# Two bottleneck blocks on one core: the second tile of block one's first convolution computed by seven half-size products inside the stream, in place of eight whole ones ahead of it

## The chip, the cores and the metric

The kernel runs on one core of one Trainium2 chip. The metric is the device time of one execution in microseconds (us); the median of several runs is compared. Engines are named as in the profile: PE (matrix products), PEld (weight loads into PE), DVE (vector), ACT (scalar activation), POOL, and SP, which here only issues transfers. All data is float32.

## The reference, cut to what matters

Two residual blocks of the same form, one after the other, on 64 images of 1024 channels and 14 x 14 pixels. The change lies in the first 1x1 convolution of block one.

```python
def block(x, w1, b1, g1, be1, w2, b2, g2, be2, w3, b3, g3, be3, residual_scale):
    out = relu(_bn(_conv(x, w1, b1, 1, 0), g1, be1))      # 1x1, 1024 -> 256 channels
    out = relu(_bn(_conv(out, w2, b2, 1, 1), g2, be2))    # 3x3, 256 -> 256
    out = _bn(_conv(out, w3, b3, 1, 0), g3, be3)          # 1x1, 256 -> 1024
    return relu(x + softplus(residual_scale)[0] * out)
x = block(x, L0 weights); x = block(x, L1 weights)
```

`_bn` normalizes each channel by its mean and variance over all images and pixels, so a convolution has to be finished on all images before what follows it can start.

## The kernel before, in words

**Tiles.** The images are taken two at a time: 32 tiles (`T`), each with 8 slices of 128 channels and 392 pixels (`PX`, the columns of a matmul). A tile is 1.6 MB and is loaded whole with one transfer (`load_x`, L104); tile zero comes in eight pieces and tile one in two. Tiles alternate between two pools of two buffers each, `x_right` and `x_left`: tiles 0 and 1 right, 2 and 3 left, 4 and 5 right, and so on. A load of a tile therefore waits until the tile four places before it has been read for the last time.

**Two ways to do the first convolution.** The 1x1 convolution is a product of a 256 x 1024 matrix with a 1024 x 392 tile. `plain_conv1` (L653) does it as eight block products: two halves of the output channels times eight slices of input channels, 16 matmuls of 392 columns. `Conv1` (L341, a `Seven`, L245) does a 2 x 2 block product with seven products in place of eight: the blocks are the two halves of output channels, the two halves of input channels, and two blocks of columns. With two tiles in a unit the blocks of columns are the two tiles, and `n` is 392; with one tile they are its two halves, and `n` is 196. Each product is four matmuls of `n` columns. For that, four sums of the weights are made once (`combine_w1`, L145; on DVE at L140) and, for each unit, four sums of the input blocks on DVE (`t3`, `t2`, `t1` in `after1`, L436, and `t4` in `after6`, L455). The seven products are `p1` to `p7`. `p1` and `p2` need no sum; `p6` needs `t2`, `p5` needs `t1`, `p7` needs `t3`, `p4` needs `t4`. Results are put together on DVE (L427) with the help of copies on ACT (L332), and DVE takes the statistics (L430).

**Order.** `stream` (L288) interlocks units: a unit's `p4` and `p3` come after the next unit's `p1`. For the first unit the order is p1, p2, p6, p5, p7; for a later one p1, then the last two of the unit before, then p6, p2, p5, p7. Matmuls, ACT work and filter steps keep the order in which they are written; where the other DVE work and the transfers go, a scheduler decides when the program is built. Between products `stream` calls `beside`, three times in the first unit and six times in a later one. Each call takes some steps of `filters` (L167), which transforms the 3x3 filters of both blocks in eight pieces of nine steps: it loads a piece (`load`, L182; the transfer is issued on SP at L185), forms sums on DVE (L192, L195), scales them on ACT and writes them to memory from POOL (L206). `calls` spreads the steps over 66 calls, eleven units' worth.

**The start.** Weights and the first tiles are loaded, the small per-channel parameters are prepared, three matmuls without use (`busy`) run, then tiles zero and one by `plain_conv1`, then 15 units of two tiles by `stream`. The last unit leads over into the 3x3 convolution (`closing`, L384). Behind it come the second convolution and the rest of both blocks, which the change leaves as they are.

Of the kernel before, what the change touches and what calls it, by code (L numbers as in the profile page):

```python
# [10 lines left out]
FP = mybir.dt.float32  # L11
# [3 lines left out]
P = 128  # L15
# [3 lines left out]
CS = C // P  # L19
MS = M // P  # L20
G = 2
T = N // G
PX = G * HW
# [46 lines left out]
def bottlenecks(ctx: ExitStack, tc: tile.TileContext, x, w1s, w2s, w3s, pars, out):  # L70
# [15 lines left out]
    def two(t, s):  # L86

        j = t % (GI // G)
        return y_grp[:, s, t // (GI // G), :, j * G * W : (j + 1) * G * W]

    class Psum:


        def __init__(self, scope, cycle, **bufs):
            self.pool = scope.enter_context(
                tc.tile_pool(name="psum", bufs=1, space=bass.MemoryType.PSUM, reuse_waits="tile")
            )
            self.cycle, self.bufs = itertools.cycle(cycle), bufs
# [17 lines left out]
    def load_w1(pool, b, queue):  # L116

        w = pool.tile([P, MS, 2, CS // 2, P], FP, tag="w1", name=f"w1_{b}")
        n = CS // 2
        for h, o in itertools.product(range(2), range(MS)):  # L120

            step = n // 2 if b == h == o == 0 else n
            for s in range(0, n, step):
                queue.dma_start(out=w[:, o, h, s : s + step], in_=w1s[b][:, o, h, s : s + step])
        return w
# [19 lines left out]
    def combine_w1(w, s):  # L145
        return combine([[w[:, o, h] for h in range(2)] for o in range(MS)], s)
# [10 lines left out]
    def matmul(*args, **kw):  # L157

        tc.keep_in_program_order(nc.tensor.matmul(*args, **kw))  # L159

    def busy(psum, tag, n, with_=None):

        v = ident if with_ is None else with_
        for i in range(n):
            matmul(psum.tile(448, tag), v, v[:, :1].to_broadcast([P, 448]), start=True, stop=True)
# [79 lines left out]
    class Seven:  # L245


        border = None
# [39 lines left out]
    def stream(items, total, beside=lambda: None, together=False):  # L288


        before = ahead = None
        items = iter(items)
        for k in range(1, total + 1):
            now = ahead if k == 2 and together else next(items)
            if k == total and now.border is not None:
                yield from now.closing(before)
                return
            if k == 1 and together:
                ahead = next(items)
                for part in now.p1, ahead.p1, now.p2, now.p6, now.p5, ahead.p6, now.p7:  # L300
                    yield from part()
                before = now
                continue
            if now is not ahead:
                yield from now.p1()
            if before is not None:
                beside()
                yield from before.last()
                beside()
            else:  # L310
                yield from now.p2()
            if now is not ahead:
                yield from now.p6()
            if before is not None:
                before.end()
                if k < total:
                    beside()
                    yield from now.p2()
            beside()
            yield from now.p5()  # L320
            beside()
            yield from now.p7()
            beside()
            if k == total:
                yield from now.p2()
            before = now
        yield from before.last()
        before.end()

    def act(*args, **kw):  # L330

        tc.keep_in_program_order(nc.scalar.activation(*args, **kw))  # L332
# [8 lines left out]
    class Conv1(Seven):  # L341
# [2 lines left out]

        prefix = "a"

        def __init__(self, psum, pool, xs, ts, w1, par, stats, border, at=None):
            self.psum, self.pool, self.ts, self.par, self.stats = psum, pool, ts, par, stats
            self.at = at = at or ts
            self.border = border if at[-1] == T - 1 else None  # L350
            self.pinned = at[-1] >= T - 1 - len(ts)
            self.a, self.s = w1
            self.n = n = len(xs) * PX // 2
            px = [slice(0, n)] * 2 if len(xs) == 2 else [slice(0, n), slice(n, 2 * n)]
            self.b = [
                [xt[:, h * CS // 2 : (h + 1) * CS // 2, p] for xt, p in zip((xs[0], xs[-1]), px)] for h in range(2)
            ]

        def sum(self, i):
            return self.pool.tile([P, CS // 2, self.n], FP, tag=f"at{i}", name=f"at{i}")  # L360

        def product(self, bank, w, b, start):
            n = CS // 2
# [2 lines left out]
                yield  # L366

        def saved(self, tag, bufs=1):
            v = self.pool.tile([P, self.n], FP, tag=tag, name=tag, bufs=bufs)
            act(v, self.y, AF.Copy)  # L370
            return v

# [110 lines left out]
    class Conv3(Seven):  # L483
# [25 lines left out]
        def part(self, row, i):  # L509
            return self.xt[:, self.o[row], i * self.n : (i + 1) * self.n]  # L510
# [150 lines left out]
    def plain_conv1(psum, t, xt, a, par, stats):  # L661

        banks = [psum.tile() for o in range(MS)]
        for h in range(2):
            for o, ps in enumerate(banks):
                for s in range(CS // 2):
                    matmul(ps, a[o][h][:, s], xt[:, h * CS // 2 + s], start=h + s == 0, stop=h + s == CS // 2)
        for o, ps in enumerate(banks):
            y = two(t, o)
            nc.scalar.activation(  # L670
                y, ps.rearrange("p (h l) -> p h l", h=H), AF.Identity, bias=par[:, B1 + o : B1 + o + 1]
            )
            nc.vector.bn_stats(stats[:, o, t, :], y)
# [1219 lines left out]
    def stats_tile(n, name):  # L1893
        return keep.tile([P, n, T, nc.vector.BN_STATS_DIM], FP, tag=f"stats{n}", name=name)
# [148 lines left out]
    par = []  # L2043
    stats1 = stats_tile(MS, "stats1_0")
# [6 lines left out]
    with tc.tile_pool(name="first", bufs=1) as one, tc.tile_pool(  # L2051
        name="first_x", bufs=2
    ) as x_left, ExitStack() as scope:
        xpools = x_right, x_left
        psum = Psum(scope, ["ps"], ps=4, ay=2)
        for i in range(1, 3):
            one.tile([P, CS // 2, PX], FP, tag=f"at{i}", name=f"at{i}")
        w1 = load_w1(one, 0, nc.scalar)
        pair = [load_x(x_right, 0, t, CS if t == 0 else 2) for t in range(2)]
        for b in range(2):  # L2060
            p = keep.tile([P, NPAR], FP, tag=f"par{b}", name=f"par{b}")
            nc.scalar.dma_start(out=p, in_=pars[b][:, :NPAR])
            par.append(p)
        sps = [softplus(p) for p in par]
        nc.scalar.activation(small.tile([P, 1], FP, tag="root", name="root"), sps[1], AF.Sqrt)
        masks.make_identity(nc, ident)
        busy(psum, "ps", 3, ones)
        w1, summed = combine_w1(w1, sums_tile(one, 1)[:, 0])
        for _ in summed:
            pass  # L2070

        border = Border(0, stats1, x_scope)
        for t, xt in enumerate(pair):
            plain_conv1(psum, t, xt, w1[0], par[0], stats1)


        spare = [y_all[:, i, NPX - CS * PX :] for i in range(MS)]
        pieces = list(itertools.product(range(2), range(MS), range(MS)))
        work = filters(pieces, spare)
        total, calls, count = FSTEPS * len(pieces), 6 * (T // 2 - 1 - CS // MS), itertools.count(1)  # L2080

        def beside():
            i = next(count)
            for _ in itertools.islice(work, total * i // calls - total * (i - 1) // calls):
                pass

        def items():
            for t in range(2, T, 2):
                xs = [load_x(xpools[t // 2 % 2], 0, t + i) for i in range(2)]
                yield Conv1(psum, one, xs, (t, t + 1), w1, par[0], stats1, border)  # L2090

        for _ in stream(items(), T // 2 - 1, beside):
            pass

    for b in range(2):
# [9 lines left out]
        with tc.tile_pool(name=f"last_{b}", bufs=1, **({"reuse_waits": "tile"} if b == 0 else {})) as one, tc.tile_pool(  # L2105
            name=f"last_x_{b}", bufs=2 if b == 0 else 5
# [3 lines left out]
            if b == 0:  # L2110
                w1, ws_a = load_w1(one, b + 1, nc.sync), sums_tile(one, 1)
# [6 lines left out]
            with ExitStack() as scope:  # L2118
                if b == 0:
                    psum = Psum(scope, ["cy"], cy=2, ay=2)  # L2120
                else:
                    psum = Psum(scope, ["cy", "cx"], cy=2, cx=2, cp=2)
# [3 lines left out]
                with tc.tile_pool(name=f"gram_{b}", bufs=1) as pool:  # L2126
                    if b == 0:
                        xs, places = [], positions()
# [9 lines left out]
                    else:  # L2138
                        homes = [x_left.tile([P, CS * PX], FP, tag="x", name="home") for _ in range(3)]
                        total = NPX // (CH * P)  # L2140
                        beside = {total - 14 + 2 * i: partial(next, summed) for i in range(4)}
# [17 lines left out]
                else:  # L2159
                    xs = [load_x(x_left, b, t, run=tc.keep_in_program_order) for t in range(5)]  # L2160
# [5 lines left out]
                with tc.tile_pool(name=f"rest_{b}", bufs=1) as pool:  # L2166
# [3 lines left out]
                    stats1 = stats_tile(MS, f"stats1_{b + 1}")  # L2170
                    border = Border(b + 1, stats1, x_scope)
# [41 lines left out]
```

## Time and profile before

| | |
|---|---|
| median of 3 runs | 1896.02 us (1895.59 to 1896.64) |
| the profiled execution | 1896.71 us, of which 1894.6 us are the span of the profile |
| PE busy, share of the span | 1876.6 us, 99% |
| DVE busy | 1574.0 us, 83% |
| ACT busy | 1092.0 us, 58% |
| POOL busy | 748.4 us, 40% |
| first matmul of tile zero | 5.72 us from the start of the span |
| first matmul of the pair 2, 3 | 27.44 us |
| first matmul of the pair 4, 5 | 40.61 us |

Times of single instructions are counted from the start of the span. A product of the program is one matmul; in the trace it is two passes, each with a weight load (PEld) of its own, so counts of PE are twice those of the code. Line numbers with an L are those of the kernel before. In a line of the timeline stand the start, the duration (or the stretch, where a line merges several), the engine, the line and the operation, the tile written and the tile read, and in brackets the idle time of the engine before and what ended it. `SPq` is SP issuing a transfer; the time is that of the issue, not of the transfer.

### The profile page before, as it was taken

What the parts mean: (1) busy time and instruction counts of PE and PEld (TensorE: products, weight loads), DVE (VectorE), ACT (ScalarE), POOL (GpSimd) and SP (SyncE); (2) the same over time, 40 slices, a digit from 0 to 9 for tenths busy, and PEclk for the clock granted to TensorE, in tenths of its full rate; (3) what the DMA queues carried; (4) which work ended last, traced back from release to release, by engine and by line L of the source; (5) the groups of instructions that cost most, each with busy time, mean ns of one, the idle gap of its engine ahead of it and who ended that gap; (6) DMA issues with size and microseconds to landing.
All of it is one profiled execution on the core that took longest, in us unless ns stands there. A gap on an engine that the chain in (4) does not pass through costs nothing. (4 is left out here: it accounts for less than half of the span.)

```text
span 1894.6 us, 28577 instructions
## 1 busy us (share of the span) xinstructions
PE 1876.6 (99%) x9778; PEld 1563.6 (83%) x9778; DVE 1574.0 (83%) x2484; ACT 1092.0 (58%) x2275; POOL 748.4 (40%) x764
## 2 busy tenths in 40 slices
PE   9999999999999999999999999999999999999999
PEld 5555557999997998899999999999999986555555
DVE  5787867999998776778878788799999986888886
ACT  2222214677777665555555555457777692666666
POOL 0111100121206555377676776501121141666665
PEclk9999999999999999999999999999999999999999
DMA  7777654797764555678788889459788467799997
GB/s 288 271 252 258 223 184 131 206 217 219 206 201 161 181 177 204 248 272 308 279 278 309 281 302 285 193 168 223 212 208 226 141 160 289 262 346 345 334 354 270
DMA packets 262369, 458.19 MB, mean 242 GB/s; under 512 B 59152, under 2 KB 228976, under 8 KB 249040
## 3 DMA queue, kind: packets, MB, share of 16 engines
q1 hardware_dynamic: 224160, 373.28, 58.8%
q0 software_dynamic: 31216, 28.81, 7.8%
q10 hardware_dynamic: 6848, 54.28, 7.1%
q8 instruction: 78, 1.28, 0.3%
q14 instruction: 67, 0.55, 0.1%
HBM read 289.44 MB, written 141.03 MB: 227 GB/s over the span
## 5 line engine op out<-in xcount | busy, mean ns | idle before, releaser
L332 ACT ACTIVATE x<-x,shift 128x392 f32<-128x392 f32 x452 | 260.0, 614 | 77.2 <-DVE x L514 31.5
L159 PE MATMUL columns<-v,ub 128*128 128x224 f32 (+1 forms) x1536 | 302.5, 338 | 1.3 <-ACT columns L332 0.8
L159 PEld LDWEIGHTS columns<-v,ub 128*128 128x128 f32 x1536 | 268.8, 188 | 7.5 <-ACT columns L332 1.5
L332 ACT ACTIVATE cu<-cy,scale 128x196 f32<-128x196 f32 (+1 forms) x360 | 175.4, 499 | 166.5 <-PE cy L159 158.9
L159 PE MATMUL ay<-at,ws 128*128 128x196 f32 (+1 forms) x768 | 192.7, 382 | 1.4 <-DVE at L440 1.4
L159 PEld LDWEIGHTS ay<-at,ws 128*128 128x128 f32 x768 | 136.1, 190 | 36.5 <-issue 1.9
L514 DVE SCALAR_TENSOR_TENSOR x<-cp,scale,x 128x196 f32<-128x196 f32 (+1 forms) x240 | 124.6, 519 | 46.1 <-PE cp L159 44.7
L645 POOL TENSOR_TENSOR x<-x,cu 128x392 f32<-128x392 f32 x120 | 125.6, 1047 | 73.3 <-DVE x L514 72.1
L332 ACT ACTIVATE au<-ay 128x196 f32<-128x196 f32 (+1 forms) x140 | 53.8, 384 | 171.8 <-PE ay L159 157.8
L159 PE MATMUL l<-diffs,ub 128*128 128x224 f32 (+1 forms) x768 | 150.2, 338 | 0.3 <-ACT sd L1934 0.3
L159 PE MATMUL m<-sums,ua 128*128 128x224 f32 (+1 forms) x752 | 145.9, 336 | 0.0
L159 PEld LDWEIGHTS l<-diffs,ub 128*128 128x128 f32 x768 | 135.2, 190 | 1.3 <-ACT sd L1934 0.6
L159 PEld LDWEIGHTS m<-sums,ua 128*128 128x128 f32 x752 | 131.5, 189 | 0.8 <-DVE sums L761 0.2
L1059 POOL DMA_DIRECT2D y<-f x24 | 32.7, 1688 | 233.7 <-DVE f L979 233.7
L537 POOL TENSOR_TENSOR x<-x,cu 128x196 f32<-128x196 f32 (+1 forms) x120 | 105.1, 875 | 47.7 <-ACT cu L332 26.2
L159 PE MATMUL cx<-y,w 128*128 128x196 f32 (+1 forms) x396 | 122.2, 394 | 1.2 <-ACT cx L332 1.2
L159 PE MATMUL cy<-y,w 128*128 128x196 f32 (+1 forms) x372 | 117.0, 402 | 0.7 <-DVE y L1461 0.7
L542 POOL TENSOR_TENSOR x<-x,cu 128x392 f32<-128x392 f32 x60 | 79.2, 1320 | 84.9 <-DVE x L514 80.7
L332 ACT ACTIVATE y<-y,shift,scale 128x1568 f32<-128x1568 f32 (+7 forms) x94 | 106.7, 1153 | 7.8 <-DVE shift L1966 6.5
L206 POOL DMA_DIRECT2D u<-y x48 | 26.0, 543 | 212.4 <-ACT y L332 211.6
L940 ACT ACTIVATE columns<-m 128x448 f32<-128x448 f32 (+1 forms) x144 | 70.8, 492 | 58.8 <-PE m L159 54.0
L1825 POOL TENSOR_SCALAR y<-y,scale 128x392 f32<-128x392 f32 x57 | 92.4, 1622 | 28.8 <-DVE scale L2156 28.2
(303 smaller groups left out, 4556.6 us busy)
## 6 DMA issues: line engine op xcount, KB each, us to landing
ub<-u SPq DMA_DIRECT2D x92, 768.0 KB, 5.2
x<-in_x SPq DMA_DIRECT2D x35, 1568.0 KB, 8.0
mid<-x ACTq DMA_DIRECT2D x32, 1568.0 KB, 9.2
x<-mid SPq DMA_DIRECT2D x32, 1568.0 KB, 9.1
out<-x SPq DMA_DIRECT2D x123, 392.0 KB, 6.9
x<-in_x SPq DMA_DIRECT2D x108, 392.0 KB, 7.8
ua<-u SPq DMA_DIRECT2D x92, 256.0 KB, 3.0
z<-kept SPq DMA_DIRECT2D x60, 392.0 KB, 3.0
```

What stands on the lines that cost most here:

```text
L159: tc.keep_in_program_order(nc.tensor.matmul(*args, **kw))
L206: nc.gpsimd.dma_start(out=us[b][i][:, s, o], in_=u)
L332: tc.keep_in_program_order(nc.scalar.activation(*args, **kw))
L514: run(nc.vector.scalar_tensor_tensor(v, bank, self.scale[:, o : o + 1], v, ALU.mult, ALU.add))
L537: run(nc.gpsimd.tensor_add(self.part(1, 1), self.part(1, 1), u3))
L542: run(nc.gpsimd.tensor_add(v, v, self.u12))
L645: nc.gpsimd.tensor_add(v, v, self.u12[:, i * self.n : (i + 1) * self.n])
L940: copy(v, m, AF.Copy)
L1059: nc.gpsimd.dma_start(out=out_rows[3][:, o], in_=fa[:, o, :full], accum_op=ALU.add)
L1825: run(nc.gpsimd.tensor_scalar(z, z, scale[:, o : o + 1], None, ALU.mult))
```

## The change

Tile one leaves `plain_conv1` and becomes the first unit of the stream: a `Conv1` of one tile, whose two blocks of columns are the tile's halves of 196. The stream now has 16 units in place of 15. Its buffers keep the size that they have for a pair (`width`), and only the first 196 columns of each are used. The rest of the stream is written as before, but since units are counted from tile one, the calls of `beside` that fell beside the pair 2, 3 now fall beside tile one, those of the pair 4, 5 beside the pair 2, 3, and so on.

```diff
-        def __init__(self, psum, pool, xs, ts, w1, par, stats, border, at=None):
+        def __init__(self, psum, pool, xs, ts, w1, par, stats, border, at=None, width=None):
...
             self.n = n = len(xs) * PX // 2
+            self.width = width or n
...
         def sum(self, i):
-            return self.pool.tile([P, CS // 2, self.n], FP, tag=f"at{i}", name=f"at{i}")
+            return self.pool.tile([P, CS // 2, self.width], FP, tag=f"at{i}", name=f"at{i}")[:, :, : self.n]
...
         def saved(self, tag, bufs=1):
-            v = self.pool.tile([P, self.n], FP, tag=tag, name=tag, bufs=bufs)
+            v = self.pool.tile([P, self.width], FP, tag=tag, name=tag, bufs=bufs)[:, : self.n]
...
-        for t, xt in enumerate(pair):
-            plain_conv1(psum, t, xt, w1[0], par[0], stats1)
+        plain_conv1(psum, 0, pair[0], w1[0], par[0], stats1)
...
         def items():
+            yield Conv1(psum, one, pair[1:], (1,), w1, par[0], stats1, border, width=PX)
             for t in range(2, T, 2):
...
-        for _ in stream(items(), T // 2 - 1, beside):
+        for _ in stream(items(), T // 2, beside):
             pass
```

## The prediction

> **What bounds the kernel now.** I read the page first: its head, the busy shares, the clock in slices and the chain.
>
> ```profile
> span 1894.6 us, 28577 instructions
> PE 1876.6 (99%) x9778; PEld 1563.6 (83%) x9778; DVE 1574.0 (83%) x2484; ACT 1092.0 (58%) x2275; POOL 748.4 (40%) x764
> ...
> PEclk9999999999999999999999999999999999999999
> ...
> PE 34%; DMA 0%; DVE 0%; SPq 0%; ACT 0%; issue 0%; DVEq 0%
> ```
>
> PE is busy for 99% of the span at the full clock, and whatever the chain names is PE. So time changes by what PE works less, plus what PE newly waits. A late PE in this stage is late to the end, since the order of its work behind the change stays the same. Next, the timeline of the first 45 us: start, duration, engine, tile written<-read, and in brackets what ended the idle time before.
>
> ```profile
> 0.76 10.13 SPq L109 DMA_DIRECT2D x<-in_x  x12
> ...
> 10.93 1.20 SPq L185 DMA_DIRECT2D y<-in_w  x2
> ...
> 13.09 0.69 DVE L140 TENSOR_TENSOR ws<-w 128x512 f32<-128x512 f32 x1
> ...
> 15.02 0.69 DVE L140 TENSOR_TENSOR ws<-w,ws 128x512 f32<-128x512 f32 x1
> ...
> 23.39 1.79 DVE L439 TENSOR_TENSOR at<-x 128x1568 f32<-128x1568 f32 x1 [5.09 <-DMA x<-in_x]
> ...
> 25.10 1.78 DVE L441 TENSOR_TENSOR at<-x,x 128x1568 f32<-128x1568 f32 x1
> 26.80 0.56 DVE L673 BATCH_NORM_STATS2 stats<-y 128x6 f32<-128x392 f32 x1
> ...
> 27.28 1.77 DVE L440 TENSOR_TENSOR at<-at,x 128x1568 f32<-128x1568 f32 x1
> 27.44 2.80 PE L159 MATMUL ay<-x,w 128*128 128x392 f32 x8
> ...
> 32.71 2.80 PE L159 MATMUL ay<-at,ws 128*128 128x392 f32 x8
> ...
> 40.61 2.80 PE L159 MATMUL ay<-x,w 128*128 128x392 f32 x8
> ```
>
> PE runs without a wait here, but the loads run hardly ahead of it. DVE sits idle until 23.39 for the load of tile three. Its three sums for the first pair (L439, L441, L440) end at 29.05, and PE reads the third at 32.71: 3.7 us of slack. The changed program uses more than that.
>
> **The change, part by part.** *Products.* A matmul stands in the trace as two passes (x counts passes). Two stretches without idle time give the price, one of 392 columns and one of 196.
>
> ```profile
> core 0: us, PE busy (x) PEld busy (x) DVE busy (x) ACT busy (x) POOL busy (x), PEclk, DMA share, GB/s
> 200.00:300.00 100.00, 100.00 (x305) 57.72 (x304) 64.56 (x85) 18.98 (x37) 6.44 (x12) 1.00 0.51 184
> 1000.00:1100.00 100.00, 100.00 (x604) 99.66 (x604) 81.80 (x155) 56.63 (x128) 69.99 (x57) 1.00 0.81 286
> ```
>
> 392 columns: 100 / 152.5 = 0.656 us. 196 columns: 100 / 302 = 0.331 us; weight loads (PEld) fill that stretch too, but add nothing. Tile one now costs 16 x 0.656 = 10.50 us, so it starts at 27.44 - 10.50 = 16.94. It will cost 28 x 0.331 = 9.27: **1.23 us less**.
>
> *What moves.* The instruction order of the built programs, engine by engine, differs in one stretch of PE, and on SP and DVE up to tiles 20 and 25; POOL is the same. What matters:
>
> ```
> PE   tile 1: p1 p2 p6 p5 p7 | pair 2,3: p1 | tile 1: p4 p3 | pair 2,3: p6 p2 p5 p7
> SP   before: x_1 x_2 x_3 in_w in_w x_4      after: x_1 in_w in_w x_2 x_3 x_4
> DVE  after: ... L428 (tile 1), L192, L440 L442 L441 (tile 3: t3, t1, t2), ...
> ```
>
> The filter steps start one unit earlier, because tile one is now the stream's first unit, and their two first loads now stand ahead of tiles two and three. (L440, L442, L441 are L439, L441, L440 of before.) I asked the DMA view for stretches that hold one issue each, and the timeline for the issue times; the last column is us to landing.
>
> ```profile
> 9.75 0.43 SPq L109 DMA_DIRECT2D x<-in_x  x1
> 10.22 0.66 SPq L109 DMA_DIRECT2D x<-in_x  x1
> 11.53 0.61 SPq L185 DMA_DIRECT2D y<-in_w  x1
> ...
> x<-in_x SPq DMA_DIRECT2D x1, 784.0 KB, 6.5
> x<-in_x SPq DMA_DIRECT2D x1, 1568.0 KB, 9.8
> x<-in_x SPq DMA_DIRECT2D x1, 1568.0 KB, 13.1
> y<-in_w SPq DMA_DIRECT2D x1, 576.0 KB, 13.9
> y<-in_w SPq DMA_DIRECT2D x1, 576.0 KB, 14.7
> ```
>
> Tile one's second half (issued near 9.4) lands at about 15.9, tile two at 9.75 + 9.8 = 19.6, tile three at 10.22 + 13.1 = 23.3, the filter loads at 10.93 + 13.9 = 24.8 and 11.53 + 14.7 = 26.2. They land in the order of issue, back to back, so the swap leaves the sum as it is: tile two should land at 19.6 + (26.2 - 23.3) = 22.5 and tile three at **26.2**.
>
> *PE up to the new wait.* Tile one from 16.94: 20 matmuls to 23.56; p1 of the pair (needs tile two, 22.5) to 26.18; tile one's p4 and p3 to **28.83**. Then p6 of the pair needs t2. DVE starts t3 when tile three lands; from the start of L439 to the end of L440, without the 0.48 us that L673 takes between, are 29.05 - 23.39 - 0.48 = 5.18 us. So t2 is ready at 26.2 + 5.2 = 31.4, and **PE waits 2.6 us**, from 28.83 to about 31.45. If tile three still landed at 23.4, t2 would be there at 28.6 and the wait would be nothing.
>
> *The two together.* p6, p2, p5, p7 take 16 x 0.656 = 10.50 from 31.45: p1 of pair 4,5 starts at 41.95, where it started at 40.61. **+1.3 us**, gain included. What stands before p6 cancels out unless it exceeds 2.6 us.
>
> *Waits inside tile one.* Its sums have 784 elements:
>
> ```profile
> L439 DVE TENSOR_TENSOR at<-x 128x784 f32<-128x784 f32 x32 | 54.3, 1696 | 0.0
> L440 DVE TENSOR_TENSOR at<-at,x 128x784 f32<-128x784 f32 x32 | 40.2, 1258 | 1.1
> L441 DVE TENSOR_TENSOR at<-x 128x784 f32<-128x784 f32 x32 | 31.2, 975 | 0.0
> ```
>
> The weight sums on L140 now end near 16.7 (15.7 plus t1's 1.0); then t3 (1.7), one L673 (0.5) and t2 (1.3) end at 20.2, against p6 of tile one at 16.94 + 8 x 0.331 = 19.6. A wait of 0 to 0.6 us, inside the 2.6: no cost. Behind t2 of the pair DVE has L192, statistics, L428 and t4; p5, 5.2 us after p6, needs the L428 that empties its bank, about 1.9 us of DVE work away: no cost. Loads: tile five waits on tile one's last product, so is issued near 28.8 in place of 27.6 and, at the 7.3 us that one took, lands at 36; its sums start when p5 has ended, past 39. Third and fourth filter loads wait on DVE steps that now come a unit earlier, with the same steps per unit: nothing, within the one wait on DVE that this stage has:
>
> ```profile
> PE ap L159 <- DVE y L427: 0.8, 1, 0.8
> ```
>
> It can go, or come twice: -0.8 to +0.8.
>
> *The clock.* This cost isn't in the sum of busy times. The waits list gives the longest waits of PE, and narrow windows the granted clock (third last column) around two of them.
>
> ```profile
> PE columns L159 <- DVE sums L761: 2.5, 2, 1.9
> PE cx L159 <- ACT cx L332: 1.2, 1, 1.2
> ...
> 598.00:600.00 2.00, 0.81 (x6) 0.79 (x6) 1.73 (x4) 1.73 (x5) 1.90 (x3) 1.00 0.97 301
> 600.00:602.00 2.00, 1.87 (x11) 1.57 (x11) 1.12 (x4) 1.49 (x5) 1.84 (x3) 1.00 0.78 252
> 1236.00:1238.00 2.00, 0.76 (x3) 0.04 (x1) 1.88 (x4) 0.68 (x2) 0.00 (x0) 1.00 0.48 160
> 1238.00:1240.00 2.00, 1.29 (x5) 1.22 (x6) 1.82 (x11) 0.70 (x3) 0.14 (x2) 0.81 1.05 339
> 1240.00:1242.00 2.00, 2.00 (x7) 1.82 (x6) 1.97 (x6) 1.77 (x3) 0.00 (x0) 0.50 1.00 344
> 1242.00:1244.00 2.00, 2.00 (x10) 1.91 (x10) 1.86 (x4) 0.57 (x4) 0.00 (x0) 0.84 0.25 89
> ```
>
> A wait of 1.2 us near 599 left the clock at 1.00. One of 1.9 us near 1237 was followed by half clock: the missing 0.19 + 0.50 + 0.16 of 2 us each, doubled, are 3.4 us at half speed, 1.7 us of work lost. Our wait of 2.6 us is longer, so I expect one such dip; part of it may fall on the wait's own end. Bounds 0 and 1.7; I take **1.5**.
>
> The Trainium skill, "TensorE: Matmul & The Clock Gate", "HAM oscillation — how this bites in real kernels", gives as the abstract rule no PE-idle gaps over about 3.4 us. By it a wait of 2.6 us would keep the clock, and the sum would end at +1.3. The dip after 1.9 us at 1237 speaks against that bound; the page's own window of 3413 ns agrees with the dip's length of 3.4 us.
>
> **Sum.** -1.23 + 2.6, rounded to +1.3, + 1.5 = +2.8 to +2.9 us. The profiled execution took 1896.71 us, 2.1 around its span of 1894.6; the median of the three runs is 1896.02. The change touches nothing around the span, so I set the sum on the median: **1898.9 us** (1899.6 on the profiled execution). About 0.2%, 3.8 us, is what a measurement of this kernel can tell from no change.
>
> **Rivals.**
>
> *B, the wait without the dip: 1896.02 + 1.3 = 1897.4.* For it: the 1.2 us wait at 599 cost no clock; a 2.6 us wait that a monitoring interval's edge halves looks like two of 1.3. Against: 1.9 us sufficed at 1237. (The skill's rule named above would lead here too.)
>
> *C, tile three isn't late: 1896.02 - 1.23 = 1894.8.* If transfers don't go strictly by issue, or the swapped loads share the engines, tile three could land near 23.4, and PE would not wait; each us of earlier landing below 26.2 gives back one. Against: the landings above keep the order of issue.
>
> *D, the loads are slower than the swap says: clearly slower.*
>
> ```profile
> 0.00:20.00 20.00, 18.93 (x48) 10.41 (x49) 6.25 (x34) 5.93 (x10) 0.71 (x6) 1.00 0.92 330
> 20.00:40.00 20.00, 20.00 (x63) 11.51 (x62) 11.85 (x11) 2.99 (x6) 0.00 (x0) 1.00 0.88 346
> ```
>
> From 15.9 on, 2 x 0.59 and 2 x 1.61 MB must land. At this stretch's mean of 346 GB/s that takes 12.7 us, tile three lands at 28.6, and the wait grows by 2.4: +3.7, with a full dip +5.4, **1901.4**. It decides from a landing past 27.2 (with the dip, over +3.8). Against: these four took 26.2 - 15.9 = 10.3 us before.
>
> **How the numbers follow.** Forecast 0.58, B 0.22, C 0.10, D 0.10. The forecast's own spread, from 0.8 either way on DVE and a dip of 1.0 to 1.7, is about 1898.0 to 1900.0. The range of 1896.6 to 1900.4 holds the forecast, nearly all of B and the near edge of D, about 0.8 in all; C and most of D are left out. Slower by over 0.2% (above 1899.8): D and the forecast's upper edge, 0.14. Faster by over 0.2% (below 1892.2): no case gives it, 0.02 for what I miss. Within: 0.84.
>
> **What would show it.** In the changed profile: the filter loads land before tile two; DVE's first 1568-element L440 starts at 26.2 (C: 23.4, D: past 27.2); PE has one new wait, on DVE `at` L441, of 2.6 us near 29 to 31; a window there shows a clock below 1.00 (B: 1.00); p1 of pair 4,5 starts 1.3 us later than 40.61, or near 43.4 with the dip. The forecast is wrong if that wait is under 1 us or over 4, or if PE gets a second wait before 170 us.

## The result, and the profile after

| | before | changed |
|---|---|---|
| median of 22 runs each | 1895.75 us | 1898.68 us |
| lowest to highest | 1894.30 to 1896.72 | 1896.42 to 1901.52 |
| span of the profiled execution | 1894.6 us | 1895.4 us |

The ratio is 1.0016, 95% interval 1.0010 to 1.0022: the change costs 2.9 us. The forecast was 1898.9. The page of the changed kernel, its head and PE's row:

```profile
span 1895.4 us, 28640 instructions
...
PE 1874.2 (99%) x9802; PEld 1568.3 (83%) x9802; DVE 1578.9 (83%) x2491; ACT 1093.4 (58%) x2277; POOL 749.6 (40%) x764
```

PE is busy for 2.4 us less than before in a span that is 0.8 us longer. What it gained it waits, and the timeline of the first 45 us says where:

```profile
9.59 1.14 SPq L185 DMA_DIRECT2D y<-in_w  x2
...
10.77 18.19 SPq L109 DMA_DIRECT2D x<-in_x  x4
...
16.52 1.49 PE L159 MATMUL ay<-x,w 128*128 128x196 f32 x8
...
23.15 2.80 PE L159 MATMUL ay<-x,w 128*128 128x392 f32 x8
...
26.00 1.79 DVE L440 TENSOR_TENSOR at<-x 128x1568 f32<-128x1568 f32 x1 [1.39 <-PE ay L159]
...
27.11 1.49 PE L159 MATMUL ap<-x,ws 128*128 128x196 f32 x8
...
27.71 1.78 DVE L442 TENSOR_TENSOR at<-x,x 128x1568 f32<-128x1568 f32 x1
...
29.41 1.78 DVE L441 TENSOR_TENSOR at<-at,x 128x1568 f32<-128x1568 f32 x1
31.11 0.69 DVE L192 TENSOR_TENSOR y<-y 128x512 f32<-128x512 f32 x1
31.34 2.87 PE L159 MATMUL ay<-at,ws 128*128 128x392 f32 x8 [2.74 <-DVE at L441]
...
34.05 2.80 PE L159 MATMUL ax<-x,w 128*128 128x392 f32 x8
...
41.95 2.80 PE L159 MATMUL ay<-x,w 128*128 128x392 f32 x8
```

The filter loads (L185) are issued ahead of tiles two and three, DVE starts the pair's first sum at 26.00 in place of 23.39, and PE, done with tile one near 28.6, waits 2.74 us for the third sum. p1 of the pair 4, 5 starts at 41.95, 1.34 us later than before.

PE could thus read the third sum 4.1 us earlier than at 32.71 before, and the fewer products are only 1.2 us of that. About 0.4 us come from tile one, which starts at 16.52 in place of 16.94, and about 2.6 from the place of the pair's p2, which reads no sum. As the stream's first unit the pair had p2 ahead of p6; as a later unit it has it behind (34.05 above). Before, it stood here:

```profile
30.08 2.80 PE L159 MATMUL ax<-x,w 128*128 128x392 f32 x8
```

The load of tile three, first in the timeline of the stretch that holds its issue alone:

```profile
11.55 0.47 SPq L109 DMA_DIRECT2D x<-in_x  x1
```

and in the DMA view of the same stretch, where the last column is us to landing:

```profile
x<-in_x SPq DMA_DIRECT2D x1, 1568.0 KB, 14.4
```

It lands at 11.55 + 14.4 = 25.9; before it was 23.3. PE's list of waits (us in total, times, the longest), first the group of the new wait, whose other two, 1.4 us, were there before; later the one on DVE that the stage had before with 0.8 us:

```profile
PE ay L159 <- DVE at L441: 4.1, 3, 2.7
...
PE ap L159 <- DVE y L428: 1.1, 1, 1.1
```

In this execution the clock didn't dip at the new wait. Of its 2.74 us, 0.76 lie ahead of 29.36 and 1.98 behind it; the clock's record in the trace has its first full-speed edge at 5.46 and its one half-clock stretch within the span at 1241.09, 3.41 us long. That is 362 steps of 3.4133 us behind the first edge, and the same steps put an edge at 29.36. The mean granted clock that is listed with each run tells the others: 6 of the 22 runs show 1.000 (median 1897.55 us), 9 show 0.999 (1898.65) and 7 show 0.998 (1900.37). One stretch of 3.41 us at half clock lowers the mean by 0.0009, so I read these as no dip, one and two: 23 / 22 = 1.05 a run. In all 14 profiles of this study that reading gives the number of dips while PE works. A half-clock stretch behind PE's last matmul can lower the mean too, by at most 0.0006 in these profiles, so a run without a profile may be counted one too high. Of the 75 runs of the kernel before that were taken beside the experiments, 42 show 1.000, 32 show 0.999 and one shows 0.998: 0.45 a run.

### The profile page after: what moved, and what is told of

Same layout as the page of the kernel before. It is cut to its first block, busy times and chain, and to the rows that moved or that the text cites. A ratio compares the mean times of both kernels' runs of the same rounds, so it can differ in the third digit from the quotient of the medians.

```text
span 1895.4 us, 28640 instructions
## 1 busy us (share of the span) xinstructions
PE 1874.2 (99%) x9802; PEld 1568.3 (83%) x9802; DVE 1578.9 (83%) x2491; ACT 1093.4 (58%) x2277; POOL 749.6 (40%) x764
## 5 line engine op out<-in xcount | busy, mean ns | idle before, releaser
L1060 POOL DMA_DIRECT2D y<-f x24 | 32.7, 1687 | 232.0 <-DVE f L980 232.0
```

The source lines that it names most:

```text
L1060: nc.gpsimd.dma_start(out=out_rows[3][:, o], in_=fa[:, o, :full], accum_op=ALU.add)
```

## The experiments

**Theory 1** is the forecast's: the filter loads make tile three late, the pair's third sum is late by as much, PE waits for it, and in part of the runs the wait costs clock. **Rival 1**: the loss comes from filter steps that run a unit earlier, not from the order of the loads. **Rival 2**: products of 196 columns, or tile one as a unit, cost more than they save. Ratios are to the kernel before, run beside each.

### Filter steps held back by one unit

```diff
         def beside():
-            i = next(count)
+            i = next(count) - 6
+            if i < 1:
+                return
```

> Seven products for tile one as in the changed kernel, but the filter steps are held back by one unit (the first six calls do nothing), so their first loads stand behind tiles two and three again and the DVE steps fall where they fell before. Theory 1 (the loss is the late landing of tile three, made late by the filter loads ahead of it): tile three lands near 23.2, t2 of the pair is ready near 28.6, PE waits under 0.3 us there, no clock dip; 1895.75 - 1.23 + 0.1 = 1894.6 us, faster than both kernels, and the 5 us spread of the changed kernel shrinks to the 2.4 us of before. Rival 2 (the products of 196 columns, or tile one as a unit of its own, cost more than they save): stays at 1896.5 or above.

1895.24 us, ratio 0.9998 (0.9989 to 1.0006), highest 1896.73. The loss is gone, and rival 2 with it. The gain isn't clear of the measurement: tile three landed at 23.3, but DVE now made t1 first and put L428 between, so that t2 ended at 29.0. PE's timeline there:

```profile
29.18 2.87 PE L159 MATMUL ay<-at,ws 128*128 128x392 f32 x8 [0.65 <-DVE at L441]
...
39.79 1.48 PE L159 MATMUL ay<-x,w 128*128 128x392 f32 x4
```

### Tiles two and three loaded first, filter steps still early

```diff
         def items():
+            early = [load_x(xpools[1], 0, 2 + i) for i in range(2)]
             yield Conv1(psum, one, pair[1:], (1,), w1, par[0], stats1, border, width=PX)
             for t in range(2, T, 2):
-                xs = [load_x(xpools[t // 2 % 2], 0, t + i) for i in range(2)]
+                xs = early if t == 2 else [load_x(xpools[t // 2 % 2], 0, t + i) for i in range(2)]
```

> The changed kernel with one thing put back: tiles two and three are loaded ahead of the first two filter loads. The filter steps stay one unit early, and two of their DVE steps now stand between t3 and t2 of the pair. Theory 1: tile three lands near 23.2, not 25.9; t2 ends near 29.7 (23.1 + two sums of 1.7 + 1.5 of filter and L428 steps + 1.8), PE waits about 1.1 us in place of 2.7, too short for a clock dip; about 1895.7 us. Rival 1 (the loss comes from filter steps that run a unit earlier beside the loads, not from the order of the loads): stays near 1898.7.

1895.87 us, ratio 1.0003 (0.9994 to 1.0012). Rival 1 expected 1898.7 and falls: with the loads in their old order, the early steps leave the time where it was before the change, so they cost no more than about the 1.2 us that the products save. The wait before p6 is 0.67 us; one of 0.33 in tile one and two of about 0.2 stand ahead of it.

```profile
28.89 1.59 PE L159 MATMUL ap<-x,ws 128*128 128x196 f32 x8 [0.21 <-DVE y L428]
31.15 2.87 PE L159 MATMUL ay<-at,ws 128*128 128x392 f32 x8 [0.67 <-DVE at L441]
```

This profile is of the slowest of the 11 runs (1897.65 us), and its first loads were late by 1.1 us (tile three at 10.42 + 14.0 = 24.4), so in a median run these waits may be shorter.

### The kernel before, with the order of loads alone

```diff
         load(pieces[0])
-        for piece, following in itertools.zip_longest(pieces, pieces[1:]):
+        load(pieces[1])
+        yield
+        for n_, (piece, following) in enumerate(itertools.zip_longest(pieces, pieces[1:])):
...
-            g = loads[-1]
+            g = loads[n_]
...
-            if following is not None:
+            if following is not None and n_:
                 load(following)
...
         work = filters(pieces, spare)
+        next(work)
```

> The kernel before (eight products for tile one) with only the order of loads of the changed kernel: the first two filter loads ahead of tiles two and three; the filter steps stay where they were. Theory 1: tile three lands near 26.1 as in the changed kernel, the sums of the pair end near 30 to 31, and PE still needs the third only at 32.7, so no wait: 1895.8 us, the same as before. A rival by which early filter loads cost time of their own (contention) gives 1897 or more.

1895.61 us, ratio 0.9999 (0.9990 to 1.0008). Tile three is as late as in the changed kernel (11.88 + 14.3 = 26.2), DVE starts as late, and PE doesn't notice:

```profile
26.25 1.79 DVE L441 TENSOR_TENSOR at<-x 128x1568 f32<-128x1568 f32 x1
...
32.76 2.80 PE L159 MATMUL ay<-at,ws 128*128 128x392 f32 x8
```

So neither the order of loads nor the new unit costs anything alone. It is both: the new unit brings p6 of the pair from 32.7 down to 28.6, into the time that the late tile takes. No run puts the pair's p2 back ahead of p6 with the loads as in the change; as an estimate, its 2.6 us would nearly fill the wait of 2.74.

### One filter load ahead in place of two

```diff
         load(pieces[0])
+        yield
         for piece, following in itertools.zip_longest(pieces, pieces[1:]):
...
         work = filters(pieces, spare)
+        next(work)
```

and the edit of `items` with `early`, as in the second experiment.

> Half the dose: the changed kernel with one of the two filter loads ahead of tiles two and three, the other behind; DVE order as in the changed kernel. Theory 1: tile three lands half way, near 24.6, t2 ends near 29.8, PE waits about 1.2 us in place of 2.7 and no dip follows; about 1895.8 us. Rival 1 (the order of the loads is not what costs): near 1898.7. A theory by which the loss hangs on DVE's work alone gives no change of the wait either.

1897.01 us, ratio 1.0004 (0.9995 to 1.0013): between, but 1.2 us above the expectation. The wait before p6 in the profile is 1.57 us, and 0.62 us are waited in tile one, whose second half landed at 16.7.

```profile
25.76 1.79 DVE L441 TENSOR_TENSOR at<-x 128x1568 f32<-128x1568 f32 x1 [0.22 <-DMA x<-in_x]
...
31.10 2.87 PE L159 MATMUL ay<-at,ws 128*128 128x392 f32 x8 [1.57 <-DVE at L442]
```

Counted from the landing of tile one's second half, tile three lands 7.5 us later with no filter load between (before, and the first experiment), 9.0 with one (16.7 to 25.7), 10.4 with two (15.5 to 25.9): the dose holds. One more profile was taken to learn where the rest of the time goes.

> The half dose once more, for one more profile: its median was 1897.0 where 1895.8 was expected, and in its first profile tile one's second half landed at 16.7 in place of 15.5 to 15.7, with everything behind it. If late first loads are what lifted its median, then with tile one at 15.6 tile three lands near 24.6, PE waits about 1.2 us, and the run takes near 1895.8; with tile one late again, the wait is 1.6 us and the run near 1897 to 1898. If the wait is 1.2 us and the run still takes 1897, something behind the pair costs time.

1897.64 us, at a mean clock of 1.000. Tile one was late again (17.4), and PE waited 1.22 us in tile one and 1.80 us before p6; p1 of the pair 4, 5 came at 42.39. And about 1.0 us more was lost near 747 us, around a wait of PE on ACT that this profile has and that of the changed kernel above hasn't:

```profile
PE ay L159 <- ACT kept L333: 0.6, 1, 0.6
```

That wait stands in five of the 14 profiles, and of one kernel's profiles in some and not in others. All four profiles known to be taken on one chip (number 7) have it, and one of the other ten. Its cause is open. Of the half dose, then, the wait is shown and the time only bracketed.

### t2 ahead of t1 on DVE, loads as in the change

```diff
         def after1(self):
...
-            run(nc.vector.tensor_sub(self.t3, self.b[1][1], self.b[0][1]))
-            run(nc.vector.tensor_add(self.t2, self.t3, self.b[0][0]))
-            run(nc.vector.tensor_sub(self.t1, self.b[0][1], self.b[0][0]))
+            keep = tc.keep_in_program_order if self.ts == (2, 3) and self.prefix == "a" and self.par is par[0] else run
+            keep(nc.vector.tensor_sub(self.t3, self.b[1][1], self.b[0][1]))
+            keep(nc.vector.tensor_add(self.t2, self.t3, self.b[0][0]))
+            keep(nc.vector.tensor_sub(self.t1, self.b[0][1], self.b[0][0]))
```

> The changed kernel, loads as they are, but DVE makes t2 of the pair ahead of t1. Theory 1: tile three still lands near 25.9; t2 ends near 30.0 in place of 31.2, since t1's 1.7 us come behind it and 0.5 us of statistics move ahead; PE waits about 1.4 us, between the 1.2 us that never cost clock and the 1.9 us that did; 1898.7 - 1.3 - 0.5 to 0.9 of dips = about 1896.7 us. A rival by which PE waits for the transfer as such and not for the third sum gives 1898.7.

1896.04 us, ratio 0.9998 (0.9989 to 1.0007), no run at 0.998. Tile three is as late behind tile one as in the change (10.4 us), yet 2.6 us of the time are back. PE waits for the third sum, not for the transfer as such: p6 starts 4.2 us behind the landing of tile three (27.84), where in the change it was 5.4. Of the other 1.4 us the dips explain about 1.2: 4 of these 11 runs show 0.999 and the rest 1.000, so 0.36 a run in place of 1.05, and one dip costs 1.7 us, as the next section shows. The wait is 1.77 us even in this profile, of the slowest run (1898.34), whose first loads were the latest of all (tile one at 17.5, with a wait of 0.89 us in tile one):

```profile
27.93 1.79 DVE L441 TENSOR_TENSOR at<-x 128x1568 f32<-128x1568 f32 x1 [1.66 <-DMA x<-in_x]
...
32.04 2.87 PE L159 MATMUL ay<-at,ws 128*128 128x392 f32 x8 [1.77 <-DVE at L442]
```

### The changed kernel twice more, for the clock

> The changed kernel once more, for one more profile. In its first profile the wait before p6 fell across two monitoring intervals (0.76 us and 1.98 us of it) and the clock stayed at 1.00. Theory 1: the dip hangs on where the wait falls; of its 22 runs 7 show a mean clock of 0.998, which none of 33 runs of before does. With the first full-speed edge at a, edges stand at a + n x 3.41 us; if over about 2.0 us of the wait lie between two of them, a half-clock stretch of 3.41 us follows at the second; if not, none. Where it does, the run takes 1899.7 or more or lacks the dip near 1240.

1898.08 us. PE's timeline in this second profile:

```profile
31.18 4.57 PE L159 MATMUL ay<-at,ws 128*128 128x392 f32 x8 [2.45 <-DVE at L441]
...
43.48 2.80 PE L159 MATMUL ay<-x,w 128*128 128x392 f32 x8
```

and its windows, with the granted clock in the third last column:

```profile
30.00:32.00 2.00, 0.82 (x2) 0.54 (x3) 2.00 (x3) 0.00 (x0) 0.00 (x0) 0.83 0.77 295
32.00:34.00 2.00, 2.00 (x5) 1.05 (x4) 2.00 (x3) 0.00 (x0) 0.00 (x0) 0.50 1.01 433
34.00:36.00 2.00, 2.00 (x6) 1.12 (x6) 1.80 (x4) 0.71 (x2) 0.00 (x0) 0.81 0.73 299
```

The whole wait, 28.73 to 31.18, lay between two edges (27.92 and 31.33); from the second on the clock is halved for 3.4 us. p6 takes 4.57 us in place of 2.87, and p1 of the pair 4, 5 starts at 43.48. From the start of p6 that is 12.30 us, where the execution without the dip took 41.95 - 31.34 = 10.61: the dip costs 1.69 us. Near 1240 this execution has no dip, and its time is under the 1899.7 us that were expected of an execution with both.

> The changed kernel a third time, for the edge of the dip. So far 2.45 us of wait within one interval of 3.41 us gave a half-clock stretch at 31.3, 1.98 us gave none, and near 1237 1.94 and 1.95 us gave one. From this run's first full-speed edge the share of the wait in one interval follows; over 2.2 us a dip at its end, under 1.9 us none. p1 of the pair 4, 5 starts near 42.0 without and near 43.5 with it.

1901.90 us, mean clock 0.998, two dips. Of a wait of 2.58 us, 2.33 lay in one interval (edges at 29.49 and 32.91), and the dip came at its end. p1 of the pair 4, 5 starts at 44.12, again 12.30 us behind p6. Timeline, then windows:

```profile
31.82 4.50 PE L159 MATMUL ay<-at,ws 128*128 128x392 f32 x8 [2.58 <-DVE at L441]
```

```profile
32.00:34.00 2.00, 2.00 (x5) 1.10 (x5) 2.00 (x4) 0.00 (x0) 0.00 (x0) 0.73 0.96 408
34.00:36.00 2.00, 2.00 (x4) 1.01 (x3) 2.00 (x4) 0.06 (x1) 0.00 (x0) 0.50 0.95 397
```

The second was near 1240 us, where the profile of before has its own. This run also had the wait near 747 us.

### The wait filled with useless matmuls

```diff
+            if k == 2:
+                fill()
             if now is not ahead:
                 yield from now.p6()
...
-        for _ in stream(items(), T // 2, beside):
+        for _ in stream(items(), T // 2, beside, fill=lambda: busy(psum, "ps", 3)):
```

Three added matmuls, which belong to no output.

> The changed kernel with three matmuls without use (448 columns, 0.75 us each, 2.2 us) put between tile one's last product and p6 of the pair, where PE waits 2.7 us. The wait stays, but PE is busy in it. Theory 1 with the clock dip as second term: start of p6 unchanged, no run with a half-clock stretch near 30 us, the median falls by the share of dips, by about 1.2 to 1897.4, and the spread falls from 5 us to about 2.5. Rival (the spread and the rest of the loss come from where the loads land, not from the clock): stays near 1898.7 with a spread of 5 us.

```profile
28.50 2.43 PE L159 MATMUL ps<-ident 128*128 128x448 f32 x6
31.46 2.87 PE L159 MATMUL ay<-at,ws 128*128 128x392 f32 x8 [0.53 <-DVE at L443]
...
42.07 2.14 PE L159 MATMUL ay<-x,w 128*128 128x392 f32 x6
```

p6 starts where it did, and no run shows 0.998. The highest falls from 1901.52 to 1898.51, but the median only to 1898.29 (ratio 1.0011, 1.0002 to 1.0019), not to 1897.4. The 11 runs lay in two clusters, so one more profile and as many runs again were taken.

> The filled wait once more, for one more profile: its 11 runs fell into two clusters, 1896.3 to 1897.1 and 1898.3 to 1898.5, with and without a dip in the mean clock in both. Near 1897: p6 of the pair starts at 31.4 to 31.5 as in its first profile. Near 1898.4: if late loads make the cluster, tile three lands past 27 and p6 starts past 32.5; if the clock does, a half-clock stretch stands near 1240 in this run and not in the others; otherwise the difference lies behind the first 60 us.

1899.65 us: tile one at 16.7, tile three at 27.1, p6 at 32.5, a dip near 1240, and the wait near 747. This one execution had the late loads, the other dip and that wait together, and lies above both clusters, so what makes the clusters stays open.

> The filled wait with as many runs again, since its first 11 fell into two clusters of five and six and its median sat in the upper one. By counts of runs the changed kernel has 1.05 dips a run (6, 9 and 7 of 22 runs at a mean clock of 1.000, 0.999 and 0.998), the kernel before 0.4. If the dip before p6 is a term of its own, 22 runs of the filled kernel together keep near 0.4 dips a run, none at 0.998, and their mean lies about 1.0 us under the 1898.9 us of the changed kernel's 22 runs; if it isn't, the mean stays at 1898.9.

1897.97 us, ratio 1.0008 (0.9999 to 1.0017). The 22 runs together: 11 at 1.000, 11 at 0.999, none at 0.998, so 0.5 dips a run; mean 1897.92, against 1898.91 for the 22 of the changed kernel. The difference of 0.99 has a standard error of 0.34 (spreads of 1.36 and 0.80). It fits the 1.05 - 0.5 = 0.55 dips a run that went, at 1.69 us each: 0.93. The sets are of different times and chips, though. Counted from the means of the kernel before beside each (1895.75 for the change, 1895.78 and 1896.45 for the two filled sets), the difference is 1.4 us.

### Steps held back and t2 ahead of t1

The first edit and the DVE edit together, meant to leave the products' gain alone.

> The filter steps held back by one unit, and t2 ahead of t1: meant to leave the gain of the products alone. Theory 1: tile three lands near 23.3, t2 ends near 27.2, PE reaches p6 of the pair near 28.5 and waits for nothing; 0.65 us less than the 1895.2 us with the steps held back alone: 1894.5 us, about 0.07% under the kernel before. Rival 2 (196 columns cost more than they save): 1895.8 or above.

1894.10 us, ratio 0.9989 (0.9981 to 0.9998): faster than both kernels, by 2.0 us against the one before run beside it. The products explain 1.23 of that; the interval reaches from 0.4 to 3.6 us, so the rest is not shown to be anything. In the profile the products' gain is all there: from tile one's first matmul to p1 of the pair 4, 5 it takes 38.94 - 16.48 = 22.46 us, before it took 40.61 - 16.94 = 23.67. Tile three lands at 10.12 + 13.1 = 23.2, and PE waits for nothing before p6:

```profile
24.02 1.78 DVE L441 TENSOR_TENSOR at<-x 128x1568 f32<-128x1568 f32 x1
25.84 1.79 DVE L442 TENSOR_TENSOR at<-at,x 128x1568 f32<-128x1568 f32 x1
...
28.40 2.80 PE L159 MATMUL ay<-at,ws 128*128 128x392 f32 x8
...
38.94 2.80 PE L159 MATMUL ay<-x,w 128*128 128x392 f32 x8
```

## Why the prediction was right, point by point

- **Products, -1.23 us.** Right. In the profile after, the 20 matmuls of p1, p2, p6, p5 and p7 of tile one take from 16.52 to 23.15, 0.331 us each.
- **Tile three at 26.2.** It landed at 25.9, and tile one's second half 0.3 us earlier than before: the swapped loads cost what they took before, in the order of issue. Rival C (not late) falls with the profiles, and so does D (past 27.2), for the changed kernel's three profiles give 25.7 to 26.4.
- **A wait of 2.6 us before p6, p1 of the pair 4, 5 at 41.95.** Measured 2.74, 2.45 and 2.58 us, and 41.95. The third sum is what PE waits for, as forecast; putting it second gives most of the loss back. That 41.95 came out to the hundredth is luck: tile three landed 0.3 us earlier than forecast and the stretch from p6 took 0.1 us longer, with PE at tile one 0.4 us earlier.
- **The clock, +1.5 us.** The mechanism was right, its size as a share of runs wrong. One dip costs 1.69 us by the profiles, near the forecast's upper bound. But I took it as coming in every run, and the first profile had none: with 2.33 and 2.45 us of the wait inside one interval it came, with 1.98 it didn't. Over the runs it is worth (1.05 - 0.45) x 1.69 = 1.0 us by dips counted, and 1.0 to 1.4 by the filled wait. Rival B had the piece that was missing, an edge that cuts the wait, but as a case of its own and not as a share of the runs.
- **All else at nothing.** Too low by about 0.5 us. The filled kernel, which has as many dips a run as the kernel before, still lies 1.7 and 1.9 us above it in the means of its two sets, not 1.3. About 0.4 of that is the wait on DVE that stood near 175 us and now stands near 158, which the forecast left at nothing within 0.8 either way: 0.8 to 1.6 us, 1.2 on average, in the ten profiles with early filter steps, 0.75 to 0.98 in the four without. What is left is within what the runs can tell. The filled kernel's two later profiles also have the wait near 747 us. Late first loads may be part of it: p6 starts 5.4 us behind tile three in all three profiles of the changed kernel, where before a slack of 3.7 us stood between. The part of the late loads is argued, not shown.
- **The sum** thus came out at 2.9 by two misses that cancel: the dip 0.5 us too high, the rest 0.5 too low.
- **Rival B (no dip, 1897.4)** describes some of the runs: the six at a mean clock of 1.000 have a median of 1897.55. It would lead there by the rule of the Trainium skill that the prediction weighed ("TensorE: Matmul & The Clock Gate", "HAM oscillation — how this bites in real kernels"). The traces differ from its 3.4 us: waits of 2.45 and 2.58 us brought the dip.

## What to carry to other kernels

Before work is taken off a busy engine, look how early its next operands are there: here a slack of 3.7 us was used up by a tile that landed 2.6 us later and a read of its sum that came 4.1 us earlier, for a saving of 1.2. Look also at what a new first unit does to the order inside the next one: the pair's p2, 2.6 us of work that needs no sum, moved behind the product that waits. When a helper's steps are counted from the first unit, a new first unit moves them all, and with them their loads past the loads that the next unit needs. A saving that turns into a wait can cost a second time through the clock, so the wait's length against the clock's interval belongs in the sum, as a cost times the share of runs in which it falls into one interval.

## What the runs showed of the hardware

**The clock's intervals.** In all 14 profiles every half-clock stretch starts a whole number of steps of 3.4133 us behind the first full-speed edge. That edge stood anywhere from 3.92 to 7.27 us after the start of the span.

**The same wait, with and without a dip.** Every profile has a wait of PE on DVE of 1.94 or 1.95 us near 1237 us. In nine of them the whole wait lay within one interval, and a dip followed at the interval's end. In the other five an edge cut it, with 1.38 to 1.80 us in the larger part, and none followed. One line of each kind, the first from the changed kernel (dip), the second from the last experiment (1.51 us in the larger part, no dip):

```profile
1239.78 2.12 PE L159 MATMUL columns<-sums,ua 128*128 128x224 f32 x8 [1.95 <-DVE sums L762]
1236.48 1.78 PE L159 MATMUL columns<-sums,ua 128*128 128x224 f32 x8 [1.95 <-DVE sums L763]
```

If an edge is as likely at one place as at another, 1.95 us lie within one interval in (3.41 - 1.95) / 3.41 = 0.43 of the runs. This estimate stands beside the 0.45 dips a run that were counted for the kernel before. For a wait of 2.6 us, with the smallest share that brings a dip somewhere between 1.98 and 2.33 us, the same working gives 0.4 to 0.6; counted were 1.05 - 0.45 = 0.60 more a run.

**Where the limit lies.** A wait of 1.98 us within one interval kept the clock near 30 us, while 1.94 us near 1237 us brought the dip. The ends of matmuls are modelled in the profile, and other matmuls stand around that wait (448 and 224 columns) than around this one. Which of the two makes the difference is not shown.

**First loads.** The landing of tile one's second half, with the same loads ahead of it, varied from 15.2 to 17.5 us between executions, by more than the products save.
